# Position logits of a two-layer attention: four copies on ScalarE first, VectorE's subtractions spread over the next two steps

## The chip, the core and the metric

The kernel runs on one core of a Trainium2 chip. A core has five engines that run beside one another, each with its own instruction queue in order: TensorE (PE in the profile; its weight loads are shown apart as PEld), VectorE (DVE), ScalarE (ACT), GpSimd (POOL) and SyncE (SP), whose queue issues the transfers here. TensorE writes its results to PSUM[...]; ScalarE and VectorE read them from there. Engines wait for one another by semaphores. The metric is the device time of one execution in microseconds; the median of three runs is 4062.5 (4062.24 to 4063.74).

## The reference

Eight images of 32 x 32 pixels with 512 channels go through two layers. With N = 1024 pixels as tokens, a layer computes x + attention(groupnorm(x)):

```
layer 0:  q, k, v = xn @ w_qkv          16 heads of 32
          out = softmax(q k^T / sqrt(32)) v @ w_proj + b_proj
layer 1:  q = xn @ Wq / sqrt(128), k = xn @ Wk, v = xn @ Wv     4 heads of 128
          scores[(x,y),(x',y')] = q . k + rel_w[x,y,y'] + rel_h[x,y,x']
          out = softmax(scores) v @ Wo
```

`rel_w[x,y,y']` is the dot product of the query at (x, y) with a learned vector that depends only on y' - y; `rel_h` is the same for x' - x. All values are 32-bit floats. This change concerns only how the two position terms are brought from PSUM to SBUF.

## The kernel before

**Tiling.** Activations are held transposed, channels on the 128 partitions and tokens along the row, in blocks of [128, 4, 1024]. Every 512 x 512 projection is done by `seven` (L328): the 2 x 2 block product with seven half-size products instead of eight, for each half of the outputs (`u`). Its products accumulate in three PSUM banks x, y and z. They come in seven steps, one `yield` each; after each, ScalarE or VectorE moves something out: x is copied (p1, L354), y + p1 becomes a (L359), x is copied to the result (c11, L398), y + p1 becomes b (L367), z is copied (p7, L373), y + p1 goes to the result (c12, L401), z + a goes to the result (c21, L404), and GpSimd adds b + p7 (c22, L408). A later product accumulates in the same bank y or z, so it waits until b or p7 has been read.

**Attention of layer 0.** `attention_0` (L506) works in 64 steps per image (4 groups of heads x 2 query halves x 8 key tiles). A step: `front` multiplies k and q for four heads into `ps`, four banks with one buffer (L513, matmuls L516); ScalarE takes the exponential of all 128 x 2048 in one instruction into `e` (L524, two buffers); `back` of the step before multiplies `e` and v into `acc` (L535), and VectorE adds `e` to the running sum `esum` (L544 for the first pair, L546 after). After eight steps `acc` is copied (L549), `finish` adds up `esum` over the partitions by matmuls with ones (L556), and `normalise` copies the sums with ScalarE (L482) and inverts them on VectorE (L484 to L500). The sums use the buffer of `acc`, so the next `acc` matmul waits for that copy.

**Position logits of layer 1.** `position_logits` (L578) makes `posT`, [128, 4, 1024]: 32 rows for the y terms (view `by_y`), 32 for the x terms (`by_x`), and the same 64 rows again for what rounding left out. `posT` has the type fp32r, a rounded float; the greater part is the rounded copy of a logit, and the rest is the logit minus that copy, so that the sum of the two is exact enough. It is done in four pieces per image. In a piece, 32 small matmuls (L592, L599) fill one bank `pp`; then, for each of four groups of 32 rows, ScalarE copies the group from `pp` into `posT` (L611, the greater part) and VectorE subtracts that copy from `pp` and writes the rest to other rows (L612). `attention_1` uses it in one matmul per score tile with the constant matrix `sel` (L627), which adds both parts.

**The order of the work.** `side_by_side` (L782) runs image b's `attention_0` as the main line and, between its steps, as many steps of other work as a cost count asks for: the projections of the image before and after, and the whole layer 1 of the image before. Every generator's `yield` gives its cost. In `second` (L728), the keys and values of layer 1 are projected (28 steps of `seven`), and `woven` (L770) puts one step of `position_logits` beside them at step 2 and every seventh from there, so at c11 of each of the four halves. The piece yields -2, so that the steps of attention come no later for it. Instructions are issued in the order in which the generators run; a scheduler then orders those that are ready and sets the semaphores. `pp` is one of the three buffers that x, y, z, and layer 1's score tiles share (`bank`, L81).

In the last round there is no `attention_0` left, and layer 1 of the eighth image runs alone.

Of the kernel before, what the change touches and what calls it, by code (L numbers as in the profile page):

```python
# [9 lines left out]
F32 = mybir.dt.float32  # L10
# [17 lines left out]
def quick_path(  # L28
# [23 lines left out]
    nc = tc.nc  # L52
# [22 lines left out]
    def block(name, shape=None, dtype=F32):  # L75
        return mem.tile(shape or [P, CC, N], dtype, tag="block", name=name, bufs=BLOCKS)

    def chunks(block):
        return [block[:, i, :] for i in range(CC)]

    def bank(name, shape=None):  # L81
        return psum.tile(shape or [P, NB], F32, tag="bank", name=name, bufs=3)
# [19 lines left out]
    for u in range(4):  # L102
        rows = slice(32 * u, 32 * u + 32)
# [54 lines left out]
    ORDER = [0, 5, 1, 4, 6, 2, 3]  # L158
# [152 lines left out]
    def forms(x, name):  # L311


        a11, a12 = x[:, :HC, :NB], x[:, HC:, :NB]
        a21, a22 = x[:, :HC, NB:], x[:, HC:, NB:]
        s1, s2, s4 = [
            mem.tile([P, HC, NB], F32, tag=f"form{i}", name=f"f{i}_{name}", bufs=1) for i in (1, 2, 4)
        ]
        nc.vector.tensor_add(s1, a21, a22)
        nc.vector.tensor_sub(s2, s1, a11)  # L320
        nc.vector.tensor_sub(a21, a11, a21)
        nc.vector.tensor_sub(s4, a12, s2)
        return [a11, a12, s4, a22, s1, s2, a21]
# [129 lines left out]
    def project_T(fs, m, y, name):  # L453

        for u in range(2):
            stream.unit(m, False, u)
            yield from seven(fs, u, False, Plain(halves(y, u)), f"{name}_{u}")

    def project_rows(fs, m, y, name, hook=None):

        for u in range(2):
            dst = [
                [y[:, h * (NT // 2) + 2 * u :, n * HN : (n + 1) * HN][:, :2] for h in range(NH)]
                for n in range(2)
            ]
            stream.unit(m, True, u)
            yield from seven(
                fs,
                u,
                True,  # L470
                Plain(dst, lambda t: t.rearrange("p (t n) -> p t n", n=HN)),
                f"{name}_{u}",
                hook if u else None,
            )
# [103 lines left out]
    def position_logits(q, posT, b):  # L578

        qv = q.rearrange("p h (x y) -> p h x y", y=IW)
        by_y = posT.rearrange("p h (x s r) -> p r s h x", r=2, s=IW // 2)
        by_x = posT.rearrange("p h (s r y) -> p r s h y", r=2, s=IH // 2)
        G = NB // (IW * H1)
        for t in range(IW // (2 * G)):
            pp = bank(f"pp_{b}_{t}", [P, G, H1, 32])
            for g in range(G):
                for r in range(2):  # L590
                    s = 2 * (t * G + g) + r
                    nc.tensor.matmul(  # L592
                        pp[64 * r : 64 * r + 32, g],
                        pw_sb[:, IW - 1 - s : 2 * IW - 1 - s],
                        qv[:, :, :, s],
                        start=True,
                        stop=True,
                    )
                    nc.tensor.matmul(  # L599
                        pp[64 * r + 32 : 64 * r + 64, g],  # L600
                        ph_sb[:, IH - 1 - s : 2 * IH - 1 - s],
                        qv[:, :, s, :],
                        start=True,
                        stop=True,
                    )
            for r in range(2):
                for u, view in enumerate((by_y, by_x)):
                    view = view[:, r, t * G : (t + 1) * G]
                    rows = slice(64 * r + 32 * u, 64 * r + 32 * u + 32)
                    rests = slice(64 * (1 - r) + 32 * u, 64 * (1 - r) + 32 * u + 32)  # L610
                    nc.scalar.copy(view[rows], pp[rows])  # L611
                    nc.vector.tensor_sub(view[rests], pp[rows], view[rows].bitcast(F32))  # L612

            yield -2

    def attention_1(q, k, v, posT, b):

# [110 lines left out]
    def second(b, st):  # L728

        fs = forms(st.pop("x1"), f"xn1_{b}")  # L730
        q = st["ao"] = block(f"q1_{b}")
        yield from project_T(fs, WQ1, chunks(q), f"q1_{b}")
        posT = block(f"posT_{b}", dtype=F32R)
        k = chunks(block(f"k1_{b}"))
        v = block(f"v1_{b}", [P, NT, C])
        keys_and_values = chain(
            project_T(fs, WK1, k, f"k1_{b}"), project_rows(fs, WV1, v, f"v1_{b}")
        )

        yield from woven(keys_and_values, position_logits(q, posT, b), 2, len(ORDER))  # L740
        st["at"] = (q, k, v, posT, b)

    def forms_1(b, st):
# [23 lines left out]
                fs, u, False, Onto(halves(xT, u), then=put_out), f"wo_{b}_{u}", hook if u else None  # L767
            )

    def woven(main, side, start, gap):  # L770

        for at, cost in enumerate(main):
            if at >= start and (at - start) % gap == 0:
                cost += next(side, 0)
            yield cost
        yield from side
# [20 lines left out]
    def chain(*parts):  # L797
        for part in parts:
            yield from part
# [47 lines left out]
    for b in range(B + 1):  # L847
        rest, total = [], 0
# [13 lines left out]
        if last is not None:  # L862
            norm = norm_1(b - 1, last)
            if here is None:
                rest.append(after_0(b - 1, last, forms_past))
                rest.append(woven(later(after_1, b - 2, past), norm, 1, 4))
            else:
                if past is not None:
                    rest.append(after_1(b - 2, past, forms_0))
                    total += PRODUCT  # L870
                rest.append(later(after_0, b - 1, last))
                rest.append(chain([ALONE], (cost + ALONE for cost in norm), marked()))
                total += PRODUCT + 3 * ALONE
            rest.append(later(second, b - 1, last))
            rest.append(woven(later(lambda st: attention_1(*st.pop("at")), last), incoming, 4, 6))
            total += SECOND
        else:
            rest.append(incoming)
# [20 lines left out]
def both_paths(tc: tile.TileContext, *args: bass.AP):  # L899
    with tc.tile_pool(name="verdict", bufs=1) as verdict:  # L900
        flag = verdict.tile([P, 1], I32, tag="flag", name="flag")
        quick_path(tc, *args, flag)
        bad = tc.nc.values_load(flag[0:1, 0:1], min_val=0, max_val=P)
        with tc.If(bad > 0):
            general_path(tc, *args)
# [474 lines left out]
```

## Time and profile before

| what | value |
|---|---|
| median of three runs | 4062.5 us |
| span of the profiled run | 4059.8 us |
| TensorE busy | 3848.8 us (95%) |
| VectorE busy | 2531.9 us (62%) |
| ScalarE busy | 1719.5 us (42%) |
| GpSimd busy | 601.6 us (15%) |
| ScalarE's position copies, L611 | 128 of 819 ns, 104.8 us |
| VectorE's position subtractions, L612 | 128 of 869 ns, 111.2 us |
| copies' idle time until a subtraction ended | 87.4 us, 96 times |
| subtractions' idle time until a copy ended | 157.3 us, 111 times |
| granted TensorE clock, mean | 0.983 |

A row of the profile's groups reads: line, engine, operation, output<-inputs by name, shapes, count; then busy time and the mean duration of one in ns; then the idle time of the engine just before these instructions, and who ended it. In timelines the columns are start and duration in microseconds, engine, line, operation, and in brackets the idle time before. PEclk is the share of TensorE's full clock that was granted.

### The profile page before, as it was taken

The numbers are of one execution on the slowest core, as the hardware profiler recorded it, in microseconds if no ns is written. First come the engines' busy times: TensorE is split into PE (matmuls) and PEld (weight loads), VectorE is DVE, ScalarE is ACT, GpSimd is POOL, SyncE is SP. The second block draws the span as 40 slices with busy tenths as digits, with TensorE's granted clock in tenths as the row PEclk, the third lists the DMA queues.
The fourth block names the chain that finished last, engine by engine and source line by source line (L and its number), as shares of the span: only waits on it lengthen the run. The fifth ranks groups of instructions, "written<-read, shape, count | busy, mean of one in ns | idle before, by whom it ended". The sixth has DMA issues, their size and how long they took to land.

```text
span 4059.8 us, 71621 instructions
## 1 busy us (share of the span) xinstructions
PE 3848.8 (95%) x30338; PEld 1417.6 (35%) x30338; DVE 2531.9 (62%) x2915; ACT 1719.5 (42%) x1761; POOL 601.6 (15%) x396
## 2 busy tenths in 40 slices
PE   6898899998999989999999999999999998999998
PEld 3232244232443324432244323433234332244353
DVE  5776665576655867458564685646856568664544
ACT  1454443444434444344443444444444444543132
POOL 1331111121111211112110111101111111111101
PEclk9999999999999999999999999999999999999999
DMA  5320120141201512014120231203311031110401
GB/s 143 118 86 26 48 59 6 37 122 50 59 6 38 129 49 58 7 47 131 37 53 12 88 85 36 53 19 95 79 37 45 26 98 54 33 63 8 115 29 22
DMA packets 498694, 234.18 MB, mean 58 GB/s; under 512 B 286368, under 2 KB 478144, under 8 KB 497344
## 3 DMA queue, kind: packets, MB, share of 16 engines
q1 hardware_dynamic: 495232, 214.79, 19.8%
q0 software_dynamic: 2608, 13.70, 0.9%
q8 instruction: 241, 3.95, 0.4%
q10 hardware_dynamic: 528, 1.05, 0.1%
q14 instruction: 85, 0.70, 0.1%
HBM read 170.72 MB, written 58.72 MB: 57 GB/s over the span
## 4 chain that ended last, share of the span: by engine, by line
PE 86%; DVE 7%; ACT 5%; issue 1%; DMA 1%; POOL 0%; SPq 0%; DVEq 0%; ACTq 0%; POOLq 0%
PE ps L516 12%; PE ps L626 11%; PE acc L638 11%; PE acc L535 11%; PE y_q L299 4%; PE y_k L299 3%; PE y_v L299 3%; PE ps L627 3%; ACT e L524 3%; PE x_v L299 3%; PE x_k L299 3%; PE x_q L299 3%; PE z_q L299 3%; PE z_v L299 2%; PE z_k L299 2%; PE y_wp L299 2%
## 5 line engine op out<-in xcount | busy, mean ns | idle before, releaser
L524 ACT ACTIVATE e<-ps 128x2048 f32<-128x2048 f32 x512 | 961.6, 1878 | 873.4 <-PE ps L516 749.1
L546 DVE TENSOR_TENSOR es<-es,e 128x2048 f32<-128x2048 f32 x384 | 899.3, 2342 | 504.5 <-ACT e L524 503.0
L516 PE MATMUL ps<-q,k 32*128 32x512 f32 x4096 | 613.1, 654 | 127.5 <-ACT e L524 127.3
L535 PE MATMUL acc<-e,v 128*32 128x512 f32 x4096 | 557.5, 617 | 12.9 <-ACT su L482 11.9
L629 ACT ACTIVATE e<-ps 128x512 f32<-128x512 f32 x512 | 305.7, 597 | 581.4 <-PE ps L627 551.2
L626 PE MATMUL ps<-q,k 128*128 128x512 f32 x1024 | 523.7, 593 | 0.0
L638 PE MATMUL acc<-e,v 128*128 128x512 f32 x1024 | 521.9, 592 | 0.0
L649 DVE TENSOR_TENSOR es<-es,e 128x512 f32<-128x512 f32 x384 | 287.0, 747 | 267.3 <-ACT e L629 266.5
L627 PE MATMUL ps<-posT,sel 128*128 128x512 f32 x512 | 406.7, 794 | 0.0
L504 POOL TENSOR_TENSOR q<-q,su 128x512 f32<-128x512 f32 x128 | 199.2, 1557 | 1381.7 <-DVE su L500 1339.3
L516 PEld LDWEIGHTS ps<-q,k 32*128 32x128 f32 x4096 | 166.6, 186 | 533.4 <-ACT e L524 267.2
L626 PEld LDWEIGHTS ps<-q,k 128*128 128x128 f32 x1024 | 193.6, 190 | 246.2 <-issue 239.4
L638 PEld LDWEIGHTS acc<-e,v 128*128 128x128 f32 x1024 | 193.1, 189 | 146.7 <-issue 105.2
L535 PEld LDWEIGHTS acc<-e,v 128*32 128x32 f32 x4096 | 82.0, 109 | 409.3 <-issue 352.1
L612 DVE TENSOR_TENSOR posT<-pp,posT 32x512 fp32r<-32x512 f32 x128 | 111.2, 869 | 157.8 <-ACT posT L611 157.3
L544 DVE TENSOR_TENSOR es<-e,e 128x2048 f32<-128x2048 f32 x64 | 173.1, 2704 | 35.7 <-ACT e L524 35.7
L484 DVE STREAM_TRANSPOSE tu<-su 128x512 f32<-128x512 f32 x128 | 90.7, 709 | 116.3 <-ACT su L482 116.0
L611 ACT CAST posT<-pp 32x512 fp32r<-32x512 f32 x128 | 104.8, 819 | 132.2 <-DVE posT L612 87.4
L482 ACT COPY su<-sums 128x512 f32<-128x512 f32 x128 | 74.9, 585 | 160.2 <-PE sums L556 92.1
L408 POOL TENSOR_TENSOR v<-b_v,p_v 128x512 f32<-128x512 f32 x32 | 67.3, 2104 | 499.8 <-ACT p_v L373 479.3
L408 POOL TENSOR_TENSOR k<-b_k,p_k 128x512 f32<-128x512 f32 x32 | 64.0, 1999 | 513.7 <-ACT p_k L373 513.7
L627 PEld LDWEIGHTS ps<-posT,sel 128*128 128x128 f32 x512 | 97.3, 190 | 122.5 <-issue 122.5
(188 smaller groups left out, 4404.1 us busy)
## 6 DMA issues: line engine op xcount, KB each, us to landing
w_qkv<-ws_qkv SPq DMA_DIRECT2D x168, 128.0 KB, 2.5
xs<-in_x SPq DMA_DIRECT2D x256, 64.0 KB, 2.6
d<-x0T SPq DMA_DIRECT2D x32, 512.0 KB, 3.0
x1T<-d SPq DMA_DIRECT2D x32, 512.0 KB, 6.4
d<-x1T SPq DMA_DIRECT2D x32, 512.0 KB, 3.6
x2T<-d SPq DMA_DIRECT2D x32, 512.0 KB, 6.0
out<-ot SPq DMA_DIRECT2D x256, 64.0 KB, 2.0
w_qkv<-in_L_conv_w_qkv SPq DMA_DIRECT2D x126, 128.0 KB, 2.2
```

The costliest lines, as they stand in the source:

```text
L299: ins = nc.tensor.matmul(out[columns, :], weights[:, columns], moving, start=start, stop=stop, skip_group_check=open_sum,)
L504: nc.gpsimd.tensor_tensor(dst, dst, su, op=ALU.mult)
L516: nc.tensor.matmul(ps[:, r, :], k[m][rows, j * P : (j + 1) * P], q[m][rows, h * NB : (h + 1) * NB], start=True, stop=True,)
L524: nc.scalar.activation(e, ps, AF.Exp, scale=D0 ** -0.5)
L535: nc.tensor.matmul(acc[r * D0 : (r + 1) * D0, :], v[:, j, c0 : c0 + D0], e[:, r, :], start=(j == 0), stop=(j == NT - 1),)
L544: nc.vector.tensor_add(state["esum"], state["first"], e)
L546: nc.vector.tensor_add(state["esum"], state["esum"], e)
L626: nc.tensor.matmul(ps, k[h][:, keys], q[:, h, queries], start=True, stop=False)
L627: nc.tensor.matmul(ps, sel[:, keys], posT[:, h, queries], start=False, stop=True)
L629: nc.scalar.activation(e, ps, AF.Exp, scale=1.0 / math.sqrt(D1))
L638: nc.tensor.matmul(acc, v[:, j, h * D1 : (h + 1) * D1], e, start=(j == 0), stop=(j == NT - 1),)
L649: nc.vector.tensor_add(state["esum"], state["esum"], e)
```

## The change

ScalarE makes the four copies of a piece one after another. The four subtractions are remembered in a list and issued later, in two parts: two at the next step of the projection, two at the one after. For this, `woven` gives the side generator a turn at three steps in a row (`places` 0, 1 and 2 after the start, modulo the gap) instead of one; other callers of `woven` keep one. The point is that ScalarE need not wait for VectorE between two copies. The arithmetic is the same, and so are all tiles.

```
@@ position_logits
+            parts = []
             for r in range(2):
                 for u, view in enumerate((by_y, by_x)):
                     view = view[:, r, t * G : (t + 1) * G]
                     rows = slice(64 * r + 32 * u, 64 * r + 32 * u + 32)
                     rests = slice(64 * (1 - r) + 32 * u, 64 * (1 - r) + 32 * u + 32)
                     nc.scalar.copy(view[rows], pp[rows])
-                    nc.vector.tensor_sub(view[rests], pp[rows], view[rows].bitcast(F32))
+                    parts.append((view[rests], pp[rows], view[rows].bitcast(F32)))
 
             yield -2
+            for i, (rest, logits, greater) in enumerate(parts):
+                nc.vector.tensor_sub(rest, logits, greater)
+                if i % 2:
+                    yield 0
@@ second
-        yield from woven(keys_and_values, position_logits(q, posT, b), 2, len(ORDER))
+        yield from woven(
+            keys_and_values, position_logits(q, posT, b), 2, len(ORDER), (0, 1, 2)
+        )
@@ woven
-    def woven(main, side, start, gap):
+    def woven(main, side, start, gap, places=(0,)):
         for at, cost in enumerate(main):
-            if at >= start and (at - start) % gap == 0:
+            if at >= start and (at - start) % gap in places:
                 cost += next(side, 0)
```

## The prediction

> **What bounds the kernel now.** I read the page first, then the list of waits, then the windows around the position pieces, then the timeline of single pieces. The page names TensorE: 3848.8 of 4059.8 us busy, so it is idle for only 211.0 us, and every microsecond that this change can win has to come out of those or out of slow matmuls.
>
> ```profile
> PE 3848.8 (95%) x30338; PEld 1417.6 (35%) x30338; DVE 2531.9 (62%) x2915; ACT 1719.5 (42%) x1761; POOL 601.6 (15%) x396
> L516 PE MATMUL ps<-q,k 32*128 32x512 f32 x4096 | 613.1, 654 | 127.5 <-ACT e L524 127.3
> L612 DVE TENSOR_TENSOR posT<-pp,posT 32x512 fp32r<-32x512 f32 x128 | 111.2, 869 | 157.8 <-ACT posT L611 157.3
> ```
>
> The second row says where TensorE idles most: the score matmuls of layer 0 wait 127.5 us for the exponential on ScalarE. The third says that VectorE's 128 subtractions wait for ScalarE's copies; the list of waits has the opposite direction too: the copies wait 87.4 us for the subtractions, 96 times. That is three times in each of 32 pieces: copy, subtraction, copy, subtraction, never two at once. One piece shows what this does to the exponential (ScalarE's timeline, then TensorE's; columns: start, duration, what, idle before and its releaser):
>
> ```profile
> 1002.60 1.06 ACT L611 CAST posT<-pp 32x512 fp32r<-32x512 f32 x1 [1.40 <-DMA w_v<-in_L_conv_Wv]
> 1004.75 0.58 ACT L611 CAST posT<-pp 32x512 fp32r<-32x512 f32 x1 [1.09 <-DVE posT L612]
> 1006.19 1.08 ACT L611 CAST posT<-pp 32x512 fp32r<-32x512 f32 x1 [0.87 <-DVE posT L612]
> 1008.36 0.58 ACT L611 CAST posT<-pp 32x512 fp32r<-32x512 f32 x1 [1.10 <-DVE posT L612]
> 1008.97 1.88 ACT L524 ACTIVATE e<-ps 128x2048 f32<-128x2048 f32 x1
> ```
>
> ```profile
> 1004.16 1.14 PE L516 MATMUL ps<-q,k 32*128 32x512 f32 x8
> 1005.23 1.06 PE L535 MATMUL acc<-e,v 128*32 128x512 f32 x8
> 1006.12 1.90 PE L299 MATMUL z_k<-x1T,w_k 128*32 128x512 f32 x16
> 1010.90 2.04 PE L516 MATMUL ps<-q,k 32*128 32x512 f32 x8 [2.88 <-ACT e L524]
> ```
>
> The scores were complete at 1005.30 (1004.16 + 1.14), but their exponential began at 1008.97, because it stands behind the fourth copy. There is one buffer for those scores (bufs=1, L513), so TensorE stops at 1008.02 for 2.88 us. The next eight score matmuls also take 2.04 us instead of the usual 1.14.
>
> How often does this happen? The windows that hold the four pieces of each of the eight images (columns: stretch, length, busy time of PE, PEld, DVE, ACT, POOL, granted clock PEclk, DMA share, GB/s):
>
> ```profile
> 494.00:590.00 96.00, 88.89 (x1016) 35.88 (x1009) 59.43 (x61) 48.86 (x48) 12.80 (x6) 0.98 0.14 39
> ...
> 3505.00:3606.00 101.00, 90.96 (x1016) 33.70 (x1008) 63.09 (x55) 54.58 (x49) 13.68 (x6) 0.97 0.11 30
> 3828.00:3885.00 57.00, 54.57 (x762) 29.41 (x755) 24.22 (x31) 20.23 (x28) 5.12 (x4) 1.00 0.30 95
> sum 679.00, PE 631.31 PEld 261.29 DVE 395.71 ACT 342.53 POOL 89.97; mean PE 78.91 PEld 32.66 DVE 49.46 ACT 42.82 POOL 11.25
> ```
>
> Length minus TensorE's busy time is 679.00 - 631.31 = 47.7 us. All of these gaps lie at a piece: in nine, TensorE waits about 2.8 us as above; in seven it waits 1.6 to 1.7 us for the copy of the sums (the 11.9 us at L535 that wait for L482), which stands in the same ScalarE queue; seven show 1.0 to 1.6 us, the last image's four 0.3 to 0.9 us, and five show none.
>
> The slow matmuls are a drop in the granted clock:
>
> ```profile
> 1011.00:1014.40 3.40, 3.40 (x16) 0.76 (x20) 2.17 (x1) 1.68 (x2) 2.90 (x1) 0.50 0.00 0
> 1994.10:2000.80 6.70, 6.08 (x28) 1.50 (x32) 4.25 (x2) 2.92 (x3) 2.90 (x1) 0.50 0.00 0
> sum 23.30, PE 22.41 PEld 5.33 DVE 15.47 ACT 11.12 POOL 14.79; mean PE 3.73 PEld 0.89 DVE 2.58 ACT 1.85 POOL 2.47
> ```
>
> Six such stretches at clock 0.50 follow pieces (from 530, 1011, 1994, 2489, 3516 and 3547 us), each right after a gap of 2.8 to 2.9 us. They hold 22.41 us of matmuls, which at full clock would take half: 11.2 us lost.
>
> [...]a drop lasts 3.4 us or a multiple, and only six of nine gaps of 2.8 us hit one[...]; gaps of 1.7 us and less at the pieces hit none. [...]copies and subtractions of one piece, which read one bank, never overlap. [...]the trace has 0.58 us for every second copy, but 1.06 us for those into the y-ordered half[...].
>
> **The change part by part.** Nothing is added or removed in arithmetic: 128 copies and 128 subtractions stay, on their engines. The built program keeps the order of TensorE, GpSimd and the DMA queue as it was; ScalarE's fourth copy comes ahead of the z copy (L373) where that had stood between, and VectorE's addition b (L367) comes ahead of the subtractions. In the built program copies two to four wait for nothing, and only the first subtraction of a piece waits for ScalarE.
>
> - *Copies back to back.* Four last 1.06 + 0.58 + 1.08 + 0.58 = 3.30 us (the mean of L611, 819 ns, gives 3.28); [...]with the 20 to 30 ns hops of the trace 3.4. I take 3.3. The fourth then ends about 1002.60 + 3.3 = 1005.9 instead of 1008.94. ScalarE comes free 3.0 us earlier in each piece.
> - *What TensorE gets of it.* The exponential runs 1005.95 to 1007.85, and TensorE wants the buffer at 1008.02: the 2.88 us close, with 0.15 us to spare. In the second kind (sums ready at 1033.7, copies from 1029.45) copies end at 1032.75, the z copy at 1033.4, the sums' copy runs 1033.7 to 1034.3, TensorE comes at 1034.75: closed. The 1 us gaps close with 2 us over. One piece (3568) keeps about 0.3 us, since its sums' copy would end at 3572.1 and TensorE is ready at 3571.8. In the last image, with no attention beside it, gaps of 0.3 us (z copy) and 0.9 us (b behind two subtractions) close as well: z's copy follows the fourth copy by then, and b goes first. I take 46 of 47.7 us; bounds 38 and 48, the lower if the 0.15 us is missed by 1 us in the nine tight pieces.
> - *Clock.* Without gaps near 2.8 us the six drops go: 11.2 us. A drop may come elsewhere, since the 8 us gaps between the images stay; I take 10, bounds 0 and 12.
> - *The later subtractions.* Before, the last one ended 7.06 us after the first copy began (1008.97 + 0.69 - 1002.60). After: 3.3 + 4 x 0.869 + hops = 6.9 us. So VectorE is done no later, and the bank is returned no later. Behind the subtractions stand the esum addition (L546) and the additions c12 and c21; the esum had to wait for the exponential until 1010.88, now VectorE is free at 1009.5. It costs nothing on the path: next x matmuls, which need a bank, came at 1019.99 and would come at 1017.1. The new wait, of the first subtraction for the fourth copy, delays only those additions, and b is ahead of it.
>
> Sum: 46 + 10 = 56 us, 4062.5 - 56 = 4006 us. TensorE takes the gain to the end, because the gaps that stay (exponential and esum between the images) are fed by its own earlier work, and the DMA wait among them (3.3 us in all for w_q) is small.
>
> **Rivals.**
> - *VectorE takes over.* In the pieces with the sums' copy, the transpose, reciprocal and first esum addition (L544) come behind the subtractions, and an exponential waits for that addition until 1040.68. They start only about 0.2 us earlier. If this takes back those seven gaps: 56 - 11.9 = 44, so 4018 us. Against it: TensorE next needs that exponential at about 1042.9, and it would end at about 1042.3.
> - *The clock drops stay*, moved to other places: 56 - 10 = 46, so 4016 us. For it: [...]longer gaps remain. Against it: at the pieces, drops stand only after gaps of 2.8 us.
> - *Gain lost later:* TensorE merely waits longer at the borders between images: about 4060 us. Against it: those waits end on ScalarE and VectorE, whose input comes from TensorE.
> - *Slower:* the position bank, one of three, is held past the next step and the x or y product waits for it. If a subtraction slipped behind an esum addition of 2.3 us, and TensorE stood for that in all 32 pieces, that is 74 us against 56 won: 4080 us. Against it: in the built order no esum addition stands between the copies and the subtractions in the pieces I followed, and the slack to the next x is 5 us with attention beside it.
>
> **How the numbers follow.** Forecast (gaps and most of the clock) 0.72; VectorE takes over 0.10; drops stay 0.10; lost later 0.04; slower 0.04. The range starts at 3998 (all 47.7 + 12, and some us of the rest) and goes to 4022, which holds both partial rivals at 4016 and 4018; what lies beyond is the last two and a lower bound of all sizes together. 0.2% is 8 us: the first three all win more, and "lost later" is no change. A larger miss on both sizes may still end within 8 us, so: faster 0.93, same 0.03, slower 0.04.
>
> **What would show it.** Right: the fourth copy ends 3.3 us after the first began, copies idle no longer for L612, the wait of L516 for the exponential falls from 127.3 us by about 32, that of L535 for the sums' copy to near nothing, length minus busy in the pieces falls from 47.7 to a few us, and no stretch at clock 0.50 follows a piece. Wrong: copies that get slower when they run one after another; a gap that remains with an esum addition or a subtraction as releaser; x products that wait for the last subtraction; new drops in the clock between images.

## The result and the profile after

The changed kernel takes 4000.89 us (median; 3999.68 to 4001.33), against 4062.37 for the kernel before on the same chip. The ratio is 0.9848 with a 95% interval of 0.9831 to 0.9865: 1.5% faster. The span of the profiled run fell from 4059.8 to 3997.9 us, by 61.9.

The page's engine line and the groups that answer to those shown of before (the copies are now L612, the subtractions L617):

```profile
PE 3830.9 (96%) x30338; PEld 1418.1 (35%) x30338; DVE 2534.3 (63%) x2915; ACT 1723.6 (43%) x1761; POOL 579.0 (14%) x396
L516 PE MATMUL ps<-q,k 32*128 32x512 f32 x4096 | 608.0, 649 | 97.3 <-ACT e L524 97.1
L535 PE MATMUL acc<-e,v 128*32 128x512 f32 x4096 | 553.9, 613 | 1.4 <-ACT e L524 1.0 <-ACT su L482 0.4
L617 DVE TENSOR_TENSOR posT<-pp,posT 32x512 fp32r<-32x512 f32 x128 | 111.7, 873 | 31.7 <-ACT posT L612 30.4
L612 ACT CAST posT<-pp 32x512 fp32r<-32x512 f32 x128 | 105.6, 825 | 46.1 <-PE pp L599 38.0 <-DMA w_v<-in_L_conv_Wv 7.0
```

The copies and subtractions take as long as before (825 and 873 ns), but no copy waits for a subtraction any more; the 87.4 us are gone. The score matmuls wait 97.1 us for the exponential instead of 127.3, and the 11.9 us in which `acc` waited for the sums' copy are 0.4.

The same piece as before in the timelines of ScalarE, VectorE and TensorE (start, duration, what, idle before):

```profile
993.23 3.36 ACT L612 CAST posT<-pp 32x512 fp32r<-32x512 f32 x4 [1.43 <-DMA w_v<-in_L_conv_Wv]
996.62 1.88 ACT L524 ACTIVATE e<-ps 128x2048 f32<-128x2048 f32 x1
```

```profile
994.95 0.69 DVE L367 TENSOR_TENSOR b_k<-y_k,p_k 128x512 f32<-128x512 f32 x1 [3.37 <-PE y_k L299]
996.62 3.52 DVE L617 TENSOR_TENSOR posT<-pp,posT 32x512 fp32r<-32x512 f32 x4 [0.98 <-ACT posT L612]
1000.17 2.72 DVE L546 TENSOR_TENSOR es<-es,e 128x2048 f32<-128x2048 f32 x1
```

```profile
994.82 1.14 PE L516 MATMUL ps<-q,k 32*128 32x512 f32 x8
995.89 1.07 PE L535 MATMUL acc<-e,v 128*32 128x512 f32 x8
996.77 1.90 PE L299 MATMUL z_k<-x1T,w_k 128*32 128x512 f32 x16
998.61 1.14 PE L516 MATMUL ps<-q,k 32*128 32x512 f32 x8
```

Four copies in one go of 3.36 us, the exponential right behind them, and TensorE goes from the z product to the next scores without a pause, at full speed (1.14 us, before 2.04). b comes ahead of the subtractions, and these end at 1000.14, 6.91 us after the first copy began.

To see where in the program the time went, I cut both traces at the same instructions: from an image's first position matmul (L592) to its first use of `posT`, eight stretches, and the rest. First three and the sum of before, then of after (columns: stretch, length, busy time of PE, PEld, DVE, ACT, POOL, PEclk, DMA share, GB/s):

```profile
494.80:586.30 91.50, 84.39 (x998) 33.77 (x991) 55.73 (x54) 46.52 (x44) 12.80 (x6) 0.98 0.13 39
1000.40:1088.10 87.70, 82.06 (x981) 32.97 (x974) 51.82 (x53) 45.21 (x44) 11.54 (x5) 0.98 0.15 42
1492.90:1579.00 86.10, 80.53 (x983) 32.79 (x975) 51.84 (x54) 44.94 (x44) 11.56 (x5) 1.00 0.16 43
...
sum 689.40, PE 641.71 PEld 263.17 DVE 405.71 ACT 348.22 POOL 90.14; mean PE 80.21 PEld 32.90 DVE 50.71 ACT 43.53 POOL 11.27
```

```profile
495.20:577.50 82.30, 82.30 (x998) 33.04 (x991) 56.56 (x54) 46.85 (x44) 9.56 (x6) 1.00 0.15 43
991.00:1071.30 80.30, 80.30 (x981) 32.84 (x974) 52.38 (x53) 45.73 (x44) 8.29 (x5) 1.00 0.17 46
1476.10:1556.50 80.40, 80.40 (x983) 32.69 (x975) 52.46 (x54) 45.83 (x44) 8.28 (x5) 1.00 0.17 46
...
sum 631.30, PE 628.91 PEld 264.98 DVE 410.28 ACT 351.97 POOL 65.68; mean PE 78.61 PEld 33.12 DVE 51.28 ACT 44.00 POOL 8.21
```

In six of the eight stretches TensorE is now busy for the whole length, at clock 1.00. They are 689.4 - 631.3 = 58.1 us shorter. Of these, TensorE's idle time gives 45.3 (689.40 - 641.71 = 47.7 before, 631.30 - 628.91 = 2.4 after), and faster matmuls 12.8 (641.71 - 628.91). That is mostly the clock: no stretch at half clock is left in the pieces, and the six of before had cost 11.2 us. All the rest of the program, some 3370 us, gives 3.8.

### The profile page after: what moved, and what is told of

Read it like the earlier page. It is cut to its first block, busy times and chain, and to the rows that moved or that the text cites. A ratio compares the mean times of both kernels' runs of the same rounds, so it can differ in the third digit from the quotient of the medians.

```text
span 3997.9 us, 71625 instructions
## 1 busy us (share of the span) xinstructions
PE 3830.9 (96%) x30338; PEld 1418.1 (35%) x30338; DVE 2534.3 (63%) x2915; ACT 1723.6 (43%) x1761; POOL 579.0 (14%) x396
## 5 line engine op out<-in xcount | busy, mean ns | idle before, releaser
L546 DVE TENSOR_TENSOR es<-es,e 128x2048 f32<-128x2048 f32 x384 | 903.4, 2352 | 450.9 <-ACT e L524 448.0
L516 PE MATMUL ps<-q,k 32*128 32x512 f32 x4096 | 608.0, 649 | 97.3 <-ACT e L524 97.1
L544 DVE TENSOR_TENSOR es<-e,e 128x2048 f32<-128x2048 f32 x64 | 172.3, 2692 | 36.1 <-ACT e L524 36.1
L652 DVE TENSOR_TENSOR es<-e,e 128x512 f32<-128x512 f32 x64 | 44.9, 701 | 145.5 <-ACT e L634 145.5
L617 DVE TENSOR_TENSOR posT<-pp,posT 32x512 fp32r<-32x512 f32 x128 | 111.7, 873 | 31.7 <-ACT posT L612 30.4
L612 ACT CAST posT<-pp 32x512 fp32r<-32x512 f32 x128 | 105.6, 825 | 46.1 <-PE pp L599 38.0
L408 POOL TENSOR_TENSOR v<-b_v,p_v 128x512 f32<-128x512 f32 x32 | 55.8, 1744 | 479.1 <-ACT p_v L373 458.5
```

Of the source, the lines that this page charges most:

```text
L516: nc.tensor.matmul(ps[:, r, :], k[m][rows, j * P : (j + 1) * P], q[m][rows, h * NB : (h + 1) * NB], start=True, stop=True,)
L544: nc.vector.tensor_add(state["esum"], state["first"], e)
L546: nc.vector.tensor_add(state["esum"], state["esum"], e)
L617: nc.vector.tensor_sub(rest, logits, greater)
```

## The experiments

My theory: only the time for which ScalarE holds up the exponential and the sums' copy counts, with the clock drops that the gaps bring. Rivals: what helps is that b comes earlier; or that the work comes in smaller portions; or VectorE now bounds the pieces. For each kernel the table gives the median, the sum of the eight stretches and TensorE's idle time in them, and the rest of the span, each from its own trace as above, with the stretches cut to the nanosecond. The program is the same in the rest for all of them, and still most of its times spread over some 6 us; so I read the pieces closely, and the rest only where it is named.

| kernel | median us | pieces us | idle in them | rest us |
|---|---|---|---|---|
| before | 4062.4 | 689.4 | 47.7 | 3370.4 |
| changed | 4000.9 | 631.3 | 2.4 | 3366.6 |
| copies first, same step | 4003.1 | 631.3 | 2.4 | 3370.0 |
| pairs spread | 4060.8 | 692.7 | 47.8 | 3369.1 |
| two copies more | 4024.9 | 652.1 | 20.6 | 3371.8 |
| copies twice | 4091.5 | 723.5 | 74.2 | 3365.6 |
| ScalarE alone held | 4107.2 | 740.7 | 76.8 | 3369.0 |
| short subtractions twice | 4019.9 | 649.9 | 17.6 | 3368.7 |
| all subtractions twice | 4083.8 | 699.6 | 53.6 | 3381.7 |

**The two halves of the change.** First the copies alone, with all subtractions in the same step (and `places` back at `(0,)`):

```
-            yield -2
-            for i, (rest, logits, greater) in enumerate(parts):
-                nc.vector.tensor_sub(rest, logits, greater)
-                if i % 2:
-                    yield 0
+            for rest, logits, greater in parts:
+                nc.vector.tensor_sub(rest, logits, greater)
+            yield -2
```

> Half of the change alone: the four copies first, but all four subtractions issued in the same step, no spreading. My theory (the gain is ScalarE's 3.0 us per piece, and the scheduler puts the addition b ahead of the subtractions anyway): 3999 to 4003 us, the same as the changed kernel within 0.1%, no gap of TensorE over 0.5 us at the pieces. Rival (spreading is needed, because b and the other VectorE work would stand behind four subtractions): TensorE waits about 2 us for b where a y product follows the z product at once, in about half of the pieces, 4025 to 4035 us.

Measured: 4003.06 us, ratio to before 0.9854 (0.9839 to 0.9869). The interval overlaps that of the changed kernel (0.9831 to 0.9865), and the pieces are the same to 0.1 us. The 2.2 us between the medians lie in the rest; the last section shows two drops of the clock there, after waits that both kernels have. Then the spreading alone, with copy and subtraction still in turn:

```
-                    nc.scalar.copy(view[rows], pp[rows])
                     parts.append(...)
             yield -2
             for i, (rest, logits, greater) in enumerate(parts):
+                nc.scalar.copy(greater, logits)
                 nc.vector.tensor_sub(rest, logits, greater)
```

> The other half alone: copy and subtraction still in turn, two pairs at each of the next two steps. My theory: the copies still wait for the subtractions three times a piece, so 4058 to 4066 us, as before the change, with 45 to 50 us of TensorE idle at the pieces and drops of the clock after gaps of 2.8 us. Rival (the gain is that ScalarE's and VectorE's work comes in smaller portions): 4000 to 4030 us.

Measured: 4060.84 us, ratio 0.9997 (0.9989 to 1.0005): no change. The copies (here L616) wait as they did before:

```profile
L616 ACT CAST posT<-pp 32x512 fp32r<-32x512 f32 x128 | 104.9, 820 | 132.6 <-DVE posT L617 87.3 <-PE pp L599 38.2 <-DMA w_v<-in_L_conv_Wv 7.1
```

So the gain at the pieces is in the order of the copies, and the two parts at later steps add nothing to it there. The traces say why. In the first of these kernels VectorE runs its 2915 instructions in the same order as in the changed one, but for one piece of the seventh image: b is ahead of the subtractions in both. b is ready while the subtractions still wait for the fourth copy, so a scheduler that places by readiness would do this; that it goes by readiness is my reading. In the second, VectorE's and ScalarE's orders are those of the kernel before, throughout. So the spreading never reached the chip, and this run doesn't show what smaller portions would do. The gain doesn't come from them, since the kernel without spreading has it.

**How much hold on ScalarE costs.** The two short copies of each piece made once more:

```
+            for rest, logits, greater in parts[1::2]:
+                nc.scalar.copy(greater.bitcast(F32R), logits)
             yield -2
```

> The changed kernel with only the two short copies of a piece made twice: ScalarE is held 1.16 us longer per piece. My theory, from the slack left in the gaps: 0.15 us slack in nine pieces, so nine gaps of 1.0 us; about 0.4 us slack in the seven with the sums' copy, so seven of 0.7; the last image's four about 1.2; no gaps near 2.8 us, so no drops of the clock: 9 + 5 + 5 = 19 us, 4015 to 4025 us. Rival A (slack is larger than I worked out): below 4008 us. Rival B (every microsecond on ScalarE counts in all 32 pieces): 37 us, 4038 us.

Measured: 4024.86 us, ratio 0.9909 (0.9893 to 0.9924), at the upper edge. One piece of TensorE's timeline:

```profile
1000.68 1.14 PE L516 MATMUL ps<-q,k 32*128 32x512 f32 x8 [1.09 <-ACT e L524]
```

The nine tight pieces show 1.04 to 1.09 us for a dose of 1.16, so the slack there is about 0.1 us (I had 0.15); six of the seven pieces with the sums' copy show 0.42 to 0.47, so 0.7 us (I had 0.4); the seventh image's shows 1.61. No clock drop follows these gaps. The 24 us over the changed kernel are 20.8 in the pieces and 5.3 in the rest. Next all four copies made twice, by the same loop over all of `parts`:

> The changed kernel with each of the four copies of a piece made twice, the second time right after the first four, so that ScalarE is held for about 6.6 us as long as it was before the change, but with work and with no wait for VectorE. My theory (only the time for which ScalarE holds up the exponential and the sums' copy counts): the gaps are back, 48 to 60 us of TensorE idle at the pieces, drops of the clock after the gaps of about 3 us, 4058 to 4080 us (the upper part if the last image's x products wait for the later subtractions). Rival (the gain came from b ahead of the subtractions, or from fewer waits by themselves): below 4015 us.

Measured: 4091.54 us, ratio 1.0075 (1.0059 to 1.009), slower than both and beyond the range. The gaps are back, longer than before (3.14 instead of 2.88, 2.53 instead of 1.72, 1.45 instead of 1.03), with ScalarE as the releaser:

```profile
1012.31 1.14 PE L516 MATMUL ps<-q,k 32*128 32x512 f32 x8 [3.14 <-ACT e L524]
```

```profile
1037.08 1.06 PE L535 MATMUL acc<-e,v 128*32 128x512 f32 x8 [2.53 <-ACT su L482]
1037.96 3.55 PE L299 MATMUL y_k<-f_xn,w_k 128*32 128x512 f32 x16
```

Idle time in the pieces is 74.2 us where I had expected 48 to 60: the eight copies hold ScalarE for 6.7 us instead of 6.3; at the sums' copy the z copy, which before ran in one of the waits between the copies, comes after them; and the last image's gaps grew from 2.4 to 12.6 us. But this kernel also delays the subtractions, which wait for the last copy, so it doesn't separate the two engines. This does: twelve short copies of a finished part of `posT` into a constant that is no longer read. No subtraction waits for them.

```
+            for _ in range(12):
+                nc.scalar.copy(ident[32:64].rearrange("p (h x) -> p h x", x=32), parts[1][2][:, 0])
             yield -2
```

> The changed kernel with twelve short copies on ScalarE after the four of a piece, from a part of the position block that is done to a constant that nobody reads any more; no VectorE instruction waits for them, so ScalarE is held longer and VectorE is not. [...] If ScalarE's hold alone makes the gaps: about that minus 0.1 us in nine pieces, minus 0.7 us in the seven with the sums' copy, and the clock drops come back: 4035 to 4070 us, with ScalarE as the releaser of the gaps. If the time of the kernel with the copies made twice came from the later subtractions: below 4012 us.

Measured: 4107.16 us, ratio 1.0106 (1.0088 to 1.0124). One piece on ScalarE, VectorE and TensorE:

```profile
1013.77 3.37 ACT L612 CAST posT<-pp 32x512 fp32r<-32x512 f32 x4 [1.43 <-DMA w_v<-in_L_conv_Wv]
1017.16 3.91 ACT L616 COPY ident<-posT 32x128 f32<-32x128 f32 x12
1021.10 1.88 ACT L524 ACTIVATE e<-ps 128x2048 f32<-128x2048 f32 x1
```

```profile
1017.17 3.46 DVE L622 TENSOR_TENSOR posT<-pp,posT 32x512 fp32r<-32x512 f32 x4 [0.98 <-ACT posT L612]
1023.01 2.29 DVE L546 TENSOR_TENSOR es<-es,e 128x2048 f32<-128x2048 f32 x1 [2.37 <-ACT e L524]
```

```profile
1023.03 1.14 PE L516 MATMUL ps<-q,k 32*128 32x512 f32 x8 [3.81 <-ACT e L524]
1024.10 1.78 PE L535 MATMUL acc<-e,v 128*32 128x512 f32 x8
```

VectorE runs all its instructions in the order of the changed kernel. The subtractions shown end 6.86 us after the first copy began (6.91 in the changed kernel), and VectorE then stands idle for 2.37 us; TensorE waits 3.81 us all the same, the dose of 3.91 minus 0.1. ScalarE's hold alone makes the gap. I missed the size, 4107 us where I had at most 4070: the dose was 3.91 us, 326 ns a copy, and my estimate of it, which rested on no trace, was smaller; the second to sixth images show five gaps each (3.8, 2.0, 0.4, 2.0, 1.4 us) where I had counted two; and the clock halves twice in each of them (as at 1024.4 here). At the sums' copy my rule, the dose minus 0.7, gives a gap of 3.2 us and it is 2.0, because there the scheduler put the sums' copy ahead of the last four of the twelve. Of the 109 us by which the pieces are longer than in the changed kernel, 74 are idle time and 35 slow matmuls.

**How much room VectorE has.** Every subtraction of the changed kernel made twice:

```
                 nc.vector.tensor_sub(rest, logits, greater)
+                nc.vector.tensor_sub(rest, logits, greater)
```

> The changed kernel with every subtraction of a piece made twice: VectorE is held 3.5 us longer per piece and gives the position bank back that much later; ScalarE's work is the same. My theory (VectorE has room): 3.5 us more in the last image's four pieces, where the next x product takes the bank at once, 14 us, and up to 2.7 us in the seven pieces with the sums' copy, where an exponential waits for the first esum addition: 4010 to 4035 us. Rival (VectorE is now what bounds the pieces): 32 x 3.5 = 111 us, 4090 to 4112 us.

Measured: 4083.8 us, ratio 1.0055 (1.0038 to 1.0071). That is 83 us more than the changed kernel for 111 us of added work on VectorE, far outside my range and nearer to the rival. By the traces, 51 us are idle time of TensorE in the pieces, 17 slower matmuls there, and 15 lie in the rest, where I can't place them. Three waits of TensorE in one image:

```profile
1016.80 1.06 PE L299 MATMUL y_k<-f_xn,w_k 128*32 128x512 f32 x8 [1.12 <-DVE k L401]
...
1041.10 1.14 PE L516 MATMUL ps<-q,k 32*128 32x512 f32 x8 [3.05 <-ACT e L524]
...
1061.57 1.72 PE L299 MATMUL x_v<-w_v,x1T 128*32 128x256 f32 x28 [1.86 <-DVE posT L618]
```

The middle one is VectorE's as well, at one remove: the first esum addition (L544) comes late, and the exponential waits for its buffer.

```profile
1036.83 2.25 DVE L544 TENSOR_TENSOR es<-e,e 128x2048 f32<-128x2048 f32 x1
```

```profile
1039.17 1.88 ACT L524 ACTIVATE e<-ps 128x2048 f32<-128x2048 f32 x1 [7.42 <-DVE es L544]
```

All eight subtractions are done by then, so the whole dose of 3.47 us stands ahead of that addition, and VectorE's slack there in the changed kernel is 3.47 - 3.05 = 0.4 us. Of these three places I had expected only this one to be overrun. The third wait can't be read in the same way, because the dose changed VectorE's order: an esum addition (L546) slipped ahead of the last subtraction, which still holds the bank.

```profile
1057.78 0.69 DVE L617 TENSOR_TENSOR posT<-pp,posT 32x512 fp32r<-32x512 f32 x1
1058.50 2.29 DVE L546 TENSOR_TENSOR es<-es,e 128x2048 f32<-128x2048 f32 x1
1060.82 0.69 DVE L618 TENSOR_TENSOR posT<-pp,posT 32x512 fp32r<-32x512 f32 x1
```

In the changed kernel the four subtractions of this piece end at 1043.52, and the next x product begins without a wait at 1047.43, so there are 3.9 us to spare:

```profile
1039.98 3.54 DVE L617 TENSOR_TENSOR posT<-pp,posT 32x512 fp32r<-32x512 f32 x4 [0.91 <-ACT posT L612]
```

```profile
1047.43 1.91 PE L299 MATMUL x_v<-w_v,x1T 128*32 128x256 f32 x32
```

The dose alone would have fitted; with the addition's 2.3 us it did not. This is the event that the prediction's rival "Slower" named. At the first wait, for c12 (L401), the dose gives 3.47 - 1.12 = 2.4 us, and the changed kernel's own timeline 1.8: c12 ends at 1006.01 there and the y product begins at 1007.77. The two esum additions ahead of c12 took 5.1 us there and 4.6 here. A smaller dose tests these slacks: the two short subtractions of each piece twice, 1.4 us.

```
                 if i % 2:
+                    nc.vector.tensor_sub(rest, logits, greater)
                     yield 0
```

> The changed kernel with the two short subtractions of a piece made twice: VectorE is held 1.4 us longer per piece. If VectorE's slack at the pieces is what the gaps of the kernel with all subtractions doubled leave of 3.5 us (0.4 us in the seven pieces with the sums' copy, 1.6 us and 2.4 us elsewhere, about 1.5 in the last image): 7 x 1.0 plus little else, 4007 to 4016 us. If VectorE has no slack: 32 x 1.4 = 44 us, 4045 us. If it has more than 1.4 us everywhere: 4000 to 4004 us.

Measured: 4019.92 us, ratio 0.9894 (0.9876 to 0.9911); 4 us over my range.

```profile
1030.06 1.14 PE L516 MATMUL ps<-q,k 32*128 32x512 f32 x8 [0.96 <-ACT e L524]
```

```profile
3810.63 1.72 PE L299 MATMUL x_v<-w_v,x1T 128*32 128x256 f32 x28 [1.71 <-DVE k L401]
```

In the first six images there is one gap each, 0.88 to 0.96 us, and nothing at the other pieces: the 0.4 us (1.38 - 0.96) holds, and the other places have room for 1.38. In the last image, with no attention beside it, I had reckoned with 1.5 us of slack and there is none: the gaps there are 1.58 to 1.71 us, while the changed kernel already has 0.2 to 0.3 there. The 1.5 came from a kernel with another order: with all subtractions twice, c12 ran ahead of the last three of the eight, and here it runs ahead of only one of six. At the piece shown, the x product waits for the end of c12 (3810.58); in the changed kernel it begins at 3791.44, just after the fourth subtraction (3791.34) and before c12 has ended. The seventh image also shows more (3.3 us once).

**The clock again.** The kernel before and the changed one were each run once more with a profile.

> The kernel before once more with a profile, for its clock record. If the drops to half clock follow the gaps of 2.8 to 2.9 us at the pieces: again about six of nine, about 22 us of matmuls at half clock there[...]; idle of TensorE at the pieces 47 to 48 us. If they come from something else, they stand at places without a gap.

Measured: 4060.6 us; idle in the pieces 689.60 - 641.84 = 47.8 us; mean clock in its first four stretches 0.98, 0.98, 1.00 and 0.96, as in the first profile. Again six of the nine gaps of 2.8 to 2.9 us are followed by a drop, with 22.9 us of matmuls at half clock in the stretches in both profiles. Two gaps of the seventh image have changed places: the one that ended at 3545.6 had a drop in the first profile and has none here (3544.4), and the one at 3603.4 had none and has one here (3600.6). So whether such a gap brings a drop differs between two runs of one program.

> The changed kernel once more with a profile. No stretch at half clock follows a piece. Outside the pieces the drops at the borders between images took 53.8 us of matmul time in its first profile against about 65 in that of before: [...]if it is part of the change, it stays within 2 us.

Measured: 3998.58 us; all eight stretches at clock 1.00 again. The drops outside the pieces took 47.0 us of matmul time instead of 53.8 (read from the trace's clock record): 6.8 us, so how long they last there changes from run to run. It moves the time by little: the rest of the span was 3365.4 us here and 3366.6 in the first.

## Why the prediction was right

- *What bounds the kernel, and the gaps.* Right. I took 46 of the 47.7 us idle at the pieces; 45.3 were won. The four copies lasted 3.3 to 3.4 us for the 3.30 reckoned. The 0.15 us to spare in the tight pieces was the thinnest number of the working; with doses of 1.16 and 3.91 us, gaps of 1.09 and 3.81 put it at 0.1. The wait of the scores for the exponential fell by 30.2 us for the 32 forecast; a gap of 0.7 us is left in the seventh image. The 0.3 us that the prediction left in one piece there are 0.4.
- *The clock.* Right in kind, a little small: I took 10 us for it, and the pieces' matmuls are 12.8 us shorter, where the six drops account for 11.2. The clock stands at 1.00 in all eight stretches. I had tied the drops to gaps near 2.8 us; in the kernel with ScalarE alone held, one of 2.03 us brought a drop as well (last section).
- *The rest.* I put it at nothing; it gave 3.8 us. 2.0 of them lie ahead of the last image's pieces (216.9 us before, 214.9 after). There the kernel before has a drop to half clock at a DMA wait of 3.3 us (of 3.0 in its second profile), and the changed kernel has none at one of 3.0 us. This is not the change: the kernel with the copies first and no spreading has the drop (216.3 us), the one with the pairs spread, whose pieces are those of before, has none (215.0). So some 2 us of the gain are luck of where the drops fall. The sum is off by -0.7 for the gaps, 2.8 for the clock and 3.8 for the rest: the 5.9 us between 56 and 61.9.
- *The subtractions end no later.* Right: 6.9 us after the first copy in forecast and trace. That VectorE is off the path holds for the change as it is, with small exceptions: gaps of 0.2 to 0.3 us in the last image, and one of 0.4 in the seventh that ends on an esum addition. My account of how far it is off the path was too generous. Of the 0.6 us that I found for the exponential behind L544 there are 0.4, and the slack of "5 us" to the next x product is 3.9 us in the piece shown above.
- *Rivals.* VectorE takes over: not with this change, but more than 0.4 us on VectorE begins it. Drops stay, gain lost later, slower: none came with the change; the esum addition ahead of a subtraction came with the dose. Of the rivals of the experiments, b's earlier place explains little: in the kernel before only two gaps of 0.9 us, both in the last image, end on b, and ScalarE's hold brings the other gaps back with b in its new place.

What the prediction did not see is that half of the change adds nothing at the pieces: the later steps had a part in its mechanism only through b, and the scheduler puts b ahead without them.

## What to carry to other kernels

When two engines read one PSUM bank in turn, see whose queue has urgent work behind the reads. Here it was ScalarE's: letting it finish all its reads first won 1.5%, and the other engine, which followed, was done no later. Price an off-path engine's hold by what stands behind it in its queue, not by its busy share: ScalarE was busy 42% of the time, and being held 3 us longer than needed cost TensorE up to 2.9. Before taking an engine for idle, put a dose of extra work on it. The dose minus the gap is the slack of a place, but only where the trace shows that the whole dose stands ahead of the wait and nothing else slipped in: at the sums' copy two doses gave the same 0.4 us, at the x product and in the last image the order had changed, and the figure was wrong.

## What the runs showed of the hardware

In these runs a gap's length alone does not tell whether the clock halves. In the kernel with the copies twice, a gap of 3.14 us (3.10 of it in the first row) left the clock at 1.00, and one of 2.53 us, 25 us later, brought 3.4 us at half clock:

```profile
1009.20:1012.30 3.10, 0.00 (x0) 0.00 (x0) 1.88 (x3) 3.05 (x4) 0.00 (x0) 1.00 0.14 42
1012.40:1015.80 3.40, 3.40 (x32) 1.03 (x36) 3.35 (x3) 2.22 (x2) 1.28 (x1) 1.00 0.00 0
1037.10:1038.00 0.90, 0.90 (x12) 0.30 (x16) 0.89 (x2) 0.90 (x1) 0.79 (x1) 1.00 0.00 0
1038.10:1041.50 3.40, 3.40 (x24) 0.49 (x12) 3.29 (x8) 0.71 (x1) 0.03 (x1) 0.50 0.02 5
```

By the traces' clock records the drops of a run begin on one grid. The kernel before has 22, from 120.121 to 4048.862 us. The distance between these two, over 1151 steps, gives 3413.3 ns a step, and all 22 lie within 1 ns of that grid; the 13 of the changed kernel lie as close to one with the same step. In the kernel with the copies twice, counted back from the drop at 1038.1, one step began at 1034.7 and holds 2.4 us of the second gap; another boundary falls at 1010.8, in the middle of the first gap, and leaves each side at most 1.6 us idle. So it seems to be TensorE's idle time within one step that counts; this is my reading of the traces. In that kernel the images follow at a period of about 494.8 us, 145 steps, and the short gap brought a drop in each of five images in a row while the long one brought none.

A step need not be idle throughout: in the kernel before, six gaps of 2.8 to 2.9 us, shorter than a step, brought drops. In the kernel with ScalarE alone held, a gap of 2.03 us that ended at 1074.56 was enough, with the drop at 1075.5. Near 1.8 us both outcomes occur. The kernel with the copies first and no spreading and the changed kernel share a wait of 1.85 us, ending at 3310.5 (1.86 us, at 3310.2); it leaves the step before 3312.1 (3311.8) idle for 1.8 us, and only the first has a drop:

```profile
3308.70:3312.10 3.40, 1.57 (x16) 0.51 (x20) 3.07 (x2) 2.08 (x2) 0.93 (x1) 0.99 0.13 39
3312.10:3315.50 3.40, 3.40 (x24) 0.81 (x16) 3.40 (x5) 1.58 (x1) 0.00 (x0) 0.50 0.00 0
```

```profile
3308.40:3311.80 3.40, 1.58 (x16) 0.52 (x20) 3.07 (x2) 2.08 (x2) 0.92 (x1) 1.00 0.13 39
3311.80:3315.20 3.40, 3.40 (x36) 0.91 (x32) 3.40 (x5) 1.57 (x1) 0.00 (x0) 1.00 0.00 0
```

That drop and the one ahead of the last image are most of the 3.4 us that these two kernels differ by in the rest. VectorE's order is the same in both up to the seventh image's pieces, which come later. Idle time within the step does not explain every drop: in the kernel before, at a border between images, a drop at 932.5 followed a step with only 1.0 us idle, and why is open.

In the kernel before and the changed one, a copy of 32 x 512 from PSUM took 0.58 us on ScalarE where its output runs along the row, and 1.01 to 1.14 us where it goes into every 32nd element. VectorE's subtractions, whose second input lies in the same way as their output, took 0.69 and 1.01 to 1.10 us.
